# Opening transfers, stage borders and the pace of side work in a two-layer pair kernel

## The chip, the cores and the metric

The kernel runs on one core of one Trainium2 chip. The metric is the device time in microseconds of one execution. Before the change it is 3307.75 us, the median of three runs (3307.7 to 3309.76). The profile was taken in an execution of its own, with a span of 3305.3 us; times of the trace count from the start of that span.

The engines are called as in the profile: PE is TensorE's matrix multiplication and PEld its weight load, DVE is VectorE, ACT is ScalarE, POOL is GpSimd, SP is SyncE, which here only issues transfers. ACT and POOL issue transfers too.

## The reference

The input x is a square table of 384 x 384 positions with 128 channels, in float32. Two layers follow each other.

The first layer is a triangle multiplication. `_layernorm(v, g, b)` subtracts the mean over channels, divides by the root of the variance plus 1e-5, multiplies by g and adds b. Then

```
z     = _layernorm(x, norm_g, norm_b)
left  = (z @ Wl + bl) * sigmoid(z @ Wlg + blg)
right = (z @ Wr + br) * sigmoid(z @ Wrg + brg)
core  = einsum('bikh,bjkh->bijh', left, right)
zo    = _layernorm(core, onorm_g, onorm_b) @ Wout + bout
x1    = x + sigmoid(x @ Wg + bg) * zo
```

so that for each of 128 channels h, `core[:, :, h]` is the product of a 384 x 384 matrix with another one transposed.

The second layer works on each row of the table:

```
left  = x1 @ W_left + b_left + x1 @ W_eq + b_eq
right = sum over the row of (x1 @ W_right + b_right)
out   = (left * right * sigmoid(x1 @ W_gate + b_gate)) @ W_out + b_out
y     = layernorm(out + x1) * ln_scale + ln_bias
```

## The kernel before, in words

One core runs three stages one after the other, with DRAM scratch between them. Within an engine every instruction stays in the order in which the program writes it (`seq`), so one that waits holds up all that stands behind it on its engine. This includes transfers that the engine issues. A transfer in the built program also waits for an earlier one whose completion semaphore it takes over; eight of these go round.

**Stage 1** (to 1140 us) makes `left` and `right` from x. x comes in chunks of 8 rows by 128 positions (`load_chunk`, 512 KB, line 115), with six buffers. A step is 4 rows, half a chunk. Per step, `stats` takes mean and variance on DVE (lines 228, 230), `powers` makes 1/sigma on POOL (243 to 246), `shift` subtracts the mean on POOL (`z`, 253), `front` transposes z on PE (262) and copies it on ACT (`zt`, 264), and `back` does, for two rows at a time, the projection on PE (`pr`, 298) with the 512 columns of the four weight matrices in `wz`, the sigmoid on ACT (305) and the product on DVE (307) into a tile `lr`. Statistics run six steps ahead (`AHEAD`); the first six are written ahead of the first `back`. The transposed x, the negative means and `lr` are stored to DRAM (`xt_d`, `nd_d`, `lr_d`). The last two `lr` tiles stay in SBUF (`kept`).

The opening must make `wz` out of the four weight matrices, the norm's g and b, and the four biases. `fold` (lines 152 to 156) forms d = b - g, multiplies a matrix of 1/128 with it and lets a matmul with the weights add the right sum over rows; `weights` (162) adds that to the scaled weights. The biases are loaded as 128 equal rows of 128 values each. The first two chunks are issued by SP; all weights, columns, biases and the next four chunks by ACT, which then loads its sigmoid table and makes the first `zt`.

**Stage 2** (1140 to 1886 us) does channel after channel, 128 of them. `load_h` brings a channel's left and right interleaved (`lrh`), `fill` takes the right half out on POOL into `rr` (lines 428, 429) and copies the kept parts (432, 433), PE does nine matmuls (449) into three PSUM banks, ACT copies them to `ct` and squares them (458, 459), DVE adds both to the sums `csum` and `csq` over channels (460, 461), and the core goes to `core_d`. `fill` runs one channel ahead. The last channel is special: its first block of 128 rows is finished first, in a bank of its own, so that the inverse deviation of rows 0 to 127 can be made at once: `variance`, `root` (ACT, line 389), `inverse` and `newton` on DVE (393, 403 to 405). Then ACT copies the other two blocks (476), and POOL adds them to the sums (478 to 480).

**Stage 3** (1886 us to the end) goes row by row. For the first 16 rows x is loaded anew (`xn`, line 510) and transposed on PE (575); after that `xt` is loaded as the negative means (`nd_d`, 516) to which POOL's own transfer adds the stored transpose (`add_x`, 524). `front` makes the gate `gT`, `scale_core` the scaled core `cs` (on DVE with a matmul that broadcasts the inverse deviation for rows 0 to 3, lines 597 and 598; on POOL after that, 600, with `rt` loaded from `rstd_d`), `layer0` the first layer's output `x1T`, `gated_left`, `layer1`, `stats1`, `norm1` and `last` the second layer (POOL takes the powers of a pair of rows at line 658 and the last addition at 690). The inverse deviations of rows 128 to 383 are made on the side, in pieces of 128 x 128 (`pieces`): six of variance, two roots taken together, six of inverse and six of Newton. From turn 16 on one is done in every turn t that divides by 5. `add_x` is called whenever 8 rows of lead have been used up.

## Time and profile before

| | |
|---|---|
| time, median of 3 | 3307.75 us |
| span of the profile | 3305.3 us |
| PE busy | 3267.0 us (99%) |
| POOL busy | 2247.9 us (68%) |
| DVE busy | 2495.4 us (75%) |
| ACT busy | 1940.4 us (59%) |
| transfers | 873.96 MB, 264 GB/s on average |

A matmul of float32 appears as two records. A "releaser" in square brackets is what ended an engine's idle time before the instruction, and the number ahead of it how long the engine had been idle. The clock column is the share of full speed that was granted to TensorE; for the first 21 us of the trace it has no entry, and shows 1.00 there whatever it was.

### The profile page before, as it was taken

How to read it: one execution, taken by the hardware profiler on the slowest of the kernel's cores; microseconds unless marked ns; L12 is line 12 of the kernel's file. 1: busy time of each engine (PE TensorE's matmuls, PEld its weight loads, DVE VectorE, ACT ScalarE, POOL GpSimd, SP SyncE). 2: the span in 40 equal slices, each digit the busy share in tenths (PEclk: the TensorE clock that was granted, in tenths of full speed). 3: DMA queues.
4: the chain of work that ended last, by engine and by line, in shares of the span. 5: the costliest groups of instructions: out<-in, count | busy, mean ns of one | idle time of the engine just before them, and what ended most of it. 6: DMA issues, size and time to landing. Idle time of an engine off the chain costs nothing.

```text
span 3305.3 us, 48361 instructions
## 1 busy us (share of the span) xinstructions
PE 3267.0 (99%) x12486; PEld 1992.0 (60%) x12486; DVE 2495.4 (75%) x8041; ACT 1940.4 (59%) x4055; POOL 2247.9 (68%) x3295
## 2 busy tenths in 40 slices
PE   8999999999999999999999999999999999999998
PEld 4544444444444466666666666666777777777776
DVE  6777777777777655555555688888888888888888
ACT  4555555555555433343334467777777777777776
POOL 5555555555555455555555579889888888888887
PEclk9999999999999999999999999999999999999999
DMA  5999999999999499999999999999999999999983
GB/s 151 267 281 268 266 279 272 264 282 271 263 279 275 130 283 283 283 281 283 284 283 282 287 296 267 264 273 276 269 280 270 275 271 276 273 272 277 271 258 113
DMA packets 922818, 873.96 MB, mean 264 GB/s; under 512 B 25008, under 2 KB 837680, under 8 KB 922544
## 3 DMA queue, kind: packets, MB, share of 16 engines
q1 hardware_dynamic: 902480, 794.13, 78.3%
q0 software_dynamic: 13248, 72.36, 11.1%
q10 hardware_dynamic: 6816, 4.39, 0.5%
q8 instruction: 102, 1.67, 0.2%
q14 instruction: 172, 1.41, 0.1%
HBM read 508.89 MB, written 361.89 MB: 263 GB/s over the span
## 4 chain that ended last, share of the span: by engine, by line
PE 62%; POOL 1%; ACT 1%; DVE 1%; issue 0%; POOLq 0%; DVEq 0%; ACTq 0%
PE pc L449 22%; PE py L638 7%; PE pr L609 7%; PE pl L627 7%; PE pg L564 7%; PE pg L626 7%; PE py L639 4%; POOL rs L658 0%; ACT py L673 0%; POOL yt L690 0%; PE pxt L575 0%; PE pq L586 0%; POOL cs L600 0%; DVE st L653 0%; ACT gT L566 0%
## 5 line engine op out<-in xcount | busy, mean ns | idle before, releaser
L298 PE MATMUL pr<-wz,zt 128*128 128x512 f32 x2304 | 1040.3, 593 | 6.2 <-DVE st L228 6.2
L305 ACT ACTIVATE sg<-pr,rs 128x256 f32<-128x256 f32 x1152 | 482.7, 470 | 499.2 <-PE pr L298 365.6
L449 PE MATMUL pc<-rr,lrh 128*128 128x384 f32 x2304 | 745.0, 487 | 2.7 <-POOL rr L428 2.7
L307 DVE SCALAR_TENSOR_TENSOR lr<-pr,rs,sg 128x256 f32<-128x256 f32 x1152 | 505.0, 480 | 267.2 <-ACT sg L305 218.8
L298 PEld LDWEIGHTS pr<-wz,zt 128*128 128x128 f32 x2304 | 414.4, 190 | 417.1 <-issue 346.0
L449 PEld LDWEIGHTS pc<-rr,lrh 128*128 128x128 f32 x2304 | 452.7, 197 | 295.0 <-POOL rr L428 3.3
L673 ACT ACTIVATE py<-py,nm,rs 128x128 f32<-128x128 f32 x1149 | 492.8, 429 | 191.6 <-POOL rs L662 126.9
L638 PEld LDWEIGHTS py<-wo,u 128*128 128x128 f32 x2304 | 377.1, 191 | 100.6 <-DVE yt L684 0.6
L460 DVE TENSOR_TENSOR csum<-csum,ct 128x1152 f32<-128x1152 f32 x127 | 175.6, 1383 | 346.6 <-ACT ct L458 346.6
L600 POOL TENSOR_TENSOR cs<-ct,rt 128x384 f32<-128x384 f32 x380 | 403.7, 1064 | 10.4 <-DMA rt<-rstd_d 9.6
L428 POOL COPY rr<-lrh 128x768 f32<-128x768 f32 x128 | 183.1, 1430 | 329.4 <-DMA lrh<-lr_d 309.2
L458 ACT COPY ct<-pc 128x1152 f32<-128x1152 f32 x127 | 142.1, 1119 | 449.4 <-PE pc L449 449.4
L638 PE MATMUL py<-wo,u 128*128 128x128 f32 x2304 | 402.7, 275 | 0.3 <-ACT wo L620 0.3
L690 POOL TENSOR_TENSOR yt<-yt,lnb 128x384 f32<-128x384 f32 x380 | 400.6, 1056 | 2.1 <-DVE yt L684 2.0
L653 DVE BATCH_NORM_STATS2 st<-py 128x6 f32<-128x128 f32 x1152 | 266.3, 287 | 84.6 <-PE py L639 82.9
L243 POOL TENSOR_SCALAR sd<-mv 128x8 f32<-128x8 f32 (+1 forms) x145 | 28.6, 197 | 436.7 <-DVE mv L230 436.6
L253 POOL TENSOR_TENSOR z<-xt,nd 128x512 f32<-128x512 f32 x288 | 299.8, 1041 | 35.9 <-POOL z L253 30.6
L609 PE MATMUL pr<-cs,wc 128*128 128x384 f32 x768 | 315.1, 492 | 0.1
L627 PE MATMUL pl<-x1T,mat_L_conv_W_left 128*128 128x384 f32 x768 | 311.4, 487 | 3.5 <-ACT gT L566 3.4
L639 PE MATMUL py<-ident,x1T 128*128 128x128 f32 x1152 | 314.0, 273 | 0.0
L626 PE MATMUL pg<-x1T,mat_L_conv_W_gate 128*128 128x384 f32 x768 | 310.8, 486 | 1.2 <-ACT g L629 1.0
L564 PE MATMUL pg<-xt,mat_L_conv_Wg 128*128 128x384 f32 x736 | 298.4, 487 | 0.0
(119 smaller groups left out, 4892.6 us busy)
## 6 DMA issues: line engine op xcount, KB each, us to landing
lr_d<-lr SPq DMA_DIRECT2D x128, 1024.0 KB, 7.1
lrh<-lr_d SPq DMA_DIRECT2D x128, 768.0 KB, 7.8
xt_d<-zt SPq DMA_DIRECT2D x288, 256.0 KB, 5.5
ct<-core_d SPq DMA_DIRECT2D x96, 768.0 KB, 4.8
rt<-rstd_d SPq DMA_DIRECT2D x95, 768.0 KB, 8.4
out_dram<-yt SPq DMA_DIRECT2D x94, 768.0 KB, 7.2
core_d<-ct SPq DMA_DIRECT2D x125, 576.0 KB, 8.9
xt<-in_x_dram SPq DMA_DIRECT2D x140, 512.0 KB, 7.0
```

The lines of the kernel that those rows point to most:

```text
L298: seq(nc.tensor.matmul(pr[:, r, :], lhsT=zts[n, q][:, 2 * half + r, :], rhs=wz, start=True, stop=True))
L305: seq(nc.scalar.activation(sg[r], pr[:, r, 2 * H:], AF.Sigmoid, scale=rs[r]))
L307: seq(nc.vector.scalar_tensor_tensor(t[:, :, c * XR + r0 + r, :], pr[:, r, :2 * H].rearrange("k (h s) -> k h s", s=2), rs[r], sg[r].rearra ...
L449: seq(nc.tensor.matmul(banks[ib], lhsT=t[:, kb, ib * P:(ib + 1) * P, 0], rhs=rr[:, kb], start=(kb == 0), stop=(kb == NB - 1),))
L564: seq(nc.tensor.matmul(pg[:, :N], lhsT=wg0, rhs=r["xT"], start=True, stop=True))
L600: seq(nc.gpsimd.tensor_tensor(cs, ct[:, i % RG], rt[:, i % RG], ALU.mult))
L609: seq(nc.tensor.matmul(pr[:, :N], lhsT=wc, rhs=r["cs"], start=True, stop=True))
L626: seq(nc.tensor.matmul(pg2[:, :N], lhsT=wgate, rhs=r["x1T"], start=True, stop=True))
L627: seq(nc.tensor.matmul(pl[:, :N], lhsT=wleft, rhs=r["x1T"], start=True, stop=True))
L638: seq(nc.tensor.matmul(py[:, s], lhsT=r["u"][:, s], rhs=r["wo"], start=True, stop=False))
L639: seq(nc.tensor.matmul(py[:, s], lhsT=r["x1T"][:, s], rhs=ident, start=False, stop=True, is_transpose=True))
L673: seq(nc.scalar.activation(py[:, s], py[:, s], AF.Identity, bias=bias, scale=scale))
```

## The change

It touches the opening, both borders and the pace of the side work. Its parts:

1. The opening issues transfers in order of need. SP brings half of the first chunk, then g and b as two rows, the other half and chunks 1 to 3; ACT brings the four weight matrices only; the four biases come as single rows, by POOL. Chunks 4 and 5 are loaded after the first step. g and b are turned from rows to columns by a matmul (`pgb`), and the bias is added by a matmul with a single row of 1/128. `fold` moves ahead of the second half of the first step's statistics, `weights` behind the first `shift`. Three matmuls without use (`busy`) keep TensorE at work meanwhile.
2. `fill` copies the kept parts first.
3. At the second border ACT copies the last two blocks ahead of the root, the store of the last channel's first block is split after 16 rows, and the inverse deviation of rows 0 to 127 is stored by POOL ahead of its three operations, no longer by SP.
4. Stage 3 loads the first rows' core as 112 and 16 partitions (channels), ahead of the fourth block of x rows. The two PSUM pools change places, so that the transposes get other banks.
5. Pieces are done in turns with t % 4 = 3 in place of every fifth, and `add_x` from turn 12 on only in turns with t % 4 = 1.

The diff, cut to its core:

```diff
-            for n in range(2):
-                load_chunk(n)
+            load_chunk(0, slice(0, 4))
...
+            for n, v in enumerate(("g", "b")):
+                load(gb[n:n + 1], a["L0_conv_norm_" + v].rearrange("(o h) -> o h", o=1))
             for n, w in enumerate(sides):
                 load(wst[:, n * H:(n + 1) * H], a["L0_conv_W" + w], nc.scalar)
-            g0, b0 = column("L0_conv_norm_g", nc.scalar), column("L0_conv_norm_b", nc.scalar)
-            for n, b in enumerate(sides):
-                load(bst[:, n * H:(n + 1) * H], a["L0_conv_b" + b].partition_broadcast(P), nc.scalar)
-            for n in range(2, 6):
-                load_chunk(n, nc.scalar)
+            load_chunk(0, slice(4, XR))
+            for n in range(1, 4):
+                load_chunk(n)
...
+            for n, b in enumerate(sides):
+                load(brow[:, n * H:(n + 1) * H], a["L0_conv_b" + b].rearrange("(o h) -> o h", o=1), nc.gpsimd)
...
+                busy(2)
+                seq(nc.tensor.matmul(pgb, lhsT=gb, rhs=ident[0:2, 0:2], start=True, stop=True))
+                seq(nc.vector.tensor_copy(g0, pgb[:, 0:1]))
+                seq(nc.vector.tensor_sub(d, pgb[:, 1:2], g0))
                 seq(nc.vector.tensor_scalar(m1, avg, d, None, ALU.mult))
-                seq(nc.tensor.matmul(p1, lhsT=m1, rhs=wst, start=True, stop=True))
-                seq(nc.vector.tensor_scalar(bst, bst, 1.0 / C, None, ALU.mult))
-                seq(nc.vector.scalar_tensor_tensor(wst, wst, g0, bst, ALU.mult, ALU.add))
+                busy(1)
+                seq(nc.tensor.matmul(p1, lhsT=m1, rhs=wst, start=True, stop=False))
+                seq(nc.tensor.matmul(p1, lhsT=avg[0:1, :], rhs=brow, start=False, stop=True))
...
                 for half in range(2):
                     stats(*steps[k], half)
+                    if k == 0 and half == 0:
+                        fold()
                 if k < AHEAD - 1:
                     powers(*steps[k])
                 if k == 0:
-                    fold()
                     zs[0] = shift(*steps[0])
+                    weights()
                     front(*steps[0], zs.pop(0))
...
-                    seq(nc.gpsimd.tensor_copy(rr[:, :NB - 1], t[:, :NB - 1, :, 1]))
-                    seq(nc.gpsimd.tensor_copy(rr[:, NB - 1, :i1], t[:, NB - 1, :i1, 1]))
                     for (kb, ig), lrt in kept.items():
                         i = slice(ig * G, (ig + 1) * G)
                         seq(nc.gpsimd.tensor_copy(t[:, kb, i, 0], lrt[:, h, :, 0]))
                         seq(nc.gpsimd.tensor_copy(rr[:, kb, i], lrt[:, h, :, 1]))
+                    seq(nc.gpsimd.tensor_copy(rr[:, :NB - 1], t[:, :NB - 1, :, 1]))
+                    seq(nc.gpsimd.tensor_copy(rr[:, NB - 1, :i1], t[:, NB - 1, :i1, 1]))
...
-                    seq(nc.scalar.dma_start(out=to[:, 0], in_=ct[:, 0]))
+                    seq(nc.scalar.dma_start(out=to[:16, 0], in_=ct[:16, 0]))
+                    seq(nc.scalar.dma_start(out=to[16:, 0], in_=ct[16:, 0]))
...
+                    seq(nc.scalar.copy(ct[:, 1:], pc[:, 1:, :N]))
                     variance(0, slice(0, N))
                     root(0)
                     inverse(0, slice(0, N))
                     newton(0, slice(0, N))
-                    seq(nc.scalar.copy(ct[:, 1:], pc[:, 1:, :N]))
                     seq(nc.scalar.dma_start(out=to[:, 1:], in_=ct[:, 1:]))
+                    seq(nc.gpsimd.dma_start(out=rstd_d[0:P, :], in_=roots[0][1]))
...
-        ps, ps2 = pool("p3ps", 4, space=PSUM), pool("p3ps2", 4, space=PSUM)
+        ps2, ps = pool("p3ps2", 4, space=PSUM), pool("p3ps", 4, space=PSUM)
...
-                seq(nc.sync.dma_start(out=ct, in_=core_d[i0:i0 + RG].rearrange("i h j -> h i j")))
+                for hs in (slice(0, H),) if i0 > 0 else (slice(0, H - 16), slice(H - 16, H)):
+                    seq(nc.sync.dma_start(out=ct[hs], in_=core_d[i0:i0 + RG, hs].rearrange("i h j -> h i j")))
...
-        for i0 in range(0, 4 * RG, RG):
+        for i0 in range(0, 3 * RG, RG):
             load_x(i0)
         load_core(0)
-        store_rstd(0)
+        load_x(3 * RG)
         load_core(RG)
...
-            if t >= 7 and added <= f + 8:
+            if t >= 7 and (t % 4 == 1 or t < 12) and added <= f + 8:
...
-            if t >= 16 and t % 5 == 0 and pieces:
+            if t >= 16 and t % 4 == 3 and pieces:
```

More of the change, by code (lines that the diff above doesn't have):

```diff
@@ L108, in triangle_then_gated_row_kernel, with load_chunk @@
             lr, full = {}, []
-            def load_chunk(n, queue=nc.sync):
+            def load_chunk(n, part=slice(0, XR)):
                 if n < len(chunks):
@@ L113, in load_chunk @@
                     i0 = ig * G + c * XR
-                    xt = xp.tile([P, XR, C], F32, tag="xt", name="xt")
-                    seq(queue.dma_start(
-                        out=xt, in_=x[i0:i0 + XR, kb * P:(kb + 1) * P, :].rearrange("i k c -> k i c")
-                    ))
-                    loaded[n] = xt
-            for n in range(2):
-                load_chunk(n)
+                    if part.start == 0:
+                        loaded[n] = xp.tile([P, XR, C], F32, tag="xt", name="xt")
+                    src = x[i0:i0 + XR, kb * P:(kb + 1) * P, :].rearrange("i k c -> k i c")
+                    seq(nc.sync.dma_start(out=loaded[n][:, part], in_=src[:, part]))
+            load_chunk(0, slice(0, 4))
             stage = lrp.tile([P, H, G, 2], F32, tag="lr", name="stage").rearrange("p h i s -> p (h i s)")
-            wst, bst = stage[:, 0:4 * H], stage[:, 4 * H:8 * H]
-            m1, d = stage[:, 8 * H:9 * H], stage[:, 9 * H:9 * H + 1]
+            wst, brow, gb = stage[:, 0:4 * H], stage[0:1, 4 * H:8 * H], stage[0:2, 8 * H:9 * H]
+            m1, d = stage[:, 9 * H:10 * H], stage[:, 10 * H:10 * H + 1]
             sides = ("l", "r", "lg", "rg")
+            for n, v in enumerate(("g", "b")):
+                load(gb[n:n + 1], a["L0_conv_norm_" + v].rearrange("(o h) -> o h", o=1))
             for n, w in enumerate(sides):
                 load(wst[:, n * H:(n + 1) * H], a["L0_conv_W" + w], nc.scalar)
-            g0, b0 = column("L0_conv_norm_g", nc.scalar), column("L0_conv_norm_b", nc.scalar)
-            for n, b in enumerate(sides):
-                load(bst[:, n * H:(n + 1) * H], a["L0_conv_b" + b].partition_broadcast(P), nc.scalar)
-            for n in range(2, 6):
-                load_chunk(n, nc.scalar)
-            ident = const([P, P], "ident")
-            make_identity(nc, ident)
+            load_chunk(0, slice(4, XR))
+            for n in range(1, 4):
+                load_chunk(n)
             avg = const([P, P], "avg")
@@ L141, in triangle_then_gated_row_kernel @@
             seq(nc.vector.memset(mhalf, -0.5))
+            ident = const([P, P], "ident")
+            make_identity(nc, ident)
+            for n, b in enumerate(sides):
+                load(brow[:, n * H:(n + 1) * H], a["L0_conv_b" + b].rearrange("(o h) -> o h", o=1), nc.gpsimd)
             warm = const([P, 1], "warm")
@@ L146, in triangle_then_gated_row_kernel, with busy @@
             p1 = pps.tile([P, 2, 4 * H], F32, tag="pr", name="p1")[:, 0]
+            pgb = tps.tile([P, 4, P], F32, tag="pt", name="pgb")[:, 0, 0:2]
+            g0 = const([P, 1], "g0")
+            def busy(n):
+                for _ in range(n):
+                    seq(nc.tensor.matmul(
+                        p1, lhsT=avg, rhs=avg.unsqueeze(1).to_broadcast([P, 4, P]), start=True, stop=True
+                    ))
             def fold():
-                seq(nc.vector.tensor_sub(d, b0, g0))
+                busy(2)
+                seq(nc.tensor.matmul(pgb, lhsT=gb, rhs=ident[0:2, 0:2], start=True, stop=True))
+                seq(nc.vector.tensor_copy(g0, pgb[:, 0:1]))
+                seq(nc.vector.tensor_sub(d, pgb[:, 1:2], g0))
                 seq(nc.vector.tensor_scalar(m1, avg, d, None, ALU.mult))
-                seq(nc.tensor.matmul(p1, lhsT=m1, rhs=wst, start=True, stop=True))
-                seq(nc.vector.tensor_scalar(bst, bst, 1.0 / C, None, ALU.mult))
-                seq(nc.vector.scalar_tensor_tensor(wst, wst, g0, bst, ALU.mult, ALU.add))
+                busy(1)
+                seq(nc.tensor.matmul(p1, lhsT=m1, rhs=wst, start=True, stop=False))
+                seq(nc.tensor.matmul(p1, lhsT=avg[0:1, :], rhs=brow, start=False, stop=True))
             def weights():
@@ L161, in weights @@
                     gs = slice(g * 2 * H, (g + 1) * 2 * H)
-                    seq(nc.vector.tensor_add(
+                    seq(nc.vector.scalar_tensor_tensor(
                         wz[:, gs].rearrange("p (h s) -> p s h", s=2),
-                        wst[:, gs].rearrange("p (s h) -> p s h", s=2),
-                        p1[:, gs].rearrange("p (s h) -> p s h", s=2),
+                        wst[:, gs].rearrange("p (s h) -> p s h", s=2), g0,
+                        p1[:, gs].rearrange("p (s h) -> p s h", s=2), ALU.mult, ALU.add,
                     ))
@@ L328, in triangle_then_gated_row_kernel @@
                 if k == 0:
-                    fold()
                     zs[0] = shift(*steps[0])
+                    weights()
                     front(*steps[0], zs.pop(0))
                 if k == 1:
-                    weights()
                     zs[1] = shift(*steps[1])
@@ L351, in triangle_then_gated_row_kernel @@
                 store_zt(n, q)
+                if k == 0:
+                    for i in range(4, 6):
+                        load_chunk(i)
                 store_slice()
```

## The prediction

> **What bounds the kernel now.** I read the busy shares first, then the idle time of TensorE (PE) in stretches, then the timelines where it is idle.

> ```profile
> PE 3267.0 (99%) x12486; PEld 1992.0 (60%) x12486; DVE 2495.4 (75%) x8041; ACT 1940.4 (59%) x4055; POOL 2247.9 (68%) x3295
> ```

> TensorE is idle for 3305.3 - 3267.0 = 38.3 us in all, so only those microseconds, and matmuls that run at a reduced clock, are to be had. The stretches show where they lie (columns: stretch, its length, then busy time and count of each engine, granted clock, DMA share, GB/s):

> ```profile
> 0.00:20.00 20.00, 4.96 (x9) 2.38 (x10) 7.41 (x41) 1.96 (x3) 6.00 (x16) 1.00 0.72 187
> ...
> 1120.00:1150.00 30.00, 27.27 (x79) 13.93 (x78) 11.82 (x25) 11.97 (x27) 8.35 (x18) 0.94 0.25 74
> ...
> 1870.00:1900.00 30.00, 27.60 (x103) 17.62 (x102) 21.53 (x22) 16.50 (x25) 11.98 (x15) 0.94 0.93 292
> ...
> 2000.00:2100.00 100.00, 97.38 (x466) 68.00 (x465) 84.47 (x302) 74.14 (x171) 86.50 (x121) 1.00 0.92 266
> 2100.00:2300.00 200.00, 198.22 (x948) 139.46 (x947) 175.06 (x615) 144.03 (x334) 178.52 (x253) 1.00 0.94 272
> ...
> 3280.00:3306.00 26.00, 11.97 (x72) 9.03 (x71) 18.12 (x67) 13.47 (x33) 13.77 (x22) 0.78 0.30 91
> ```

> Idle: 15.0 us in the opening, 2.7 at the first border (stage 1 to 2), 2.4 at the second, 2.6 + 1.8 early in stage 3, 13.3 in the tail, which the change leaves alone. Everywhere else TensorE is full. In the timeline of the opening (start, duration, engine, line), watch what the first projection (L298) waits for:

> ```profile
> 5.42 0.49 DVE L228 BATCH_NORM_STATS2 st<-xt 128x6 f32<-128x128 f32 x2 [4.40 <-DMA xt<-in_x_dram]
> ...
> 8.30 7.62 ACTq L115 DMA_DIRECT2D xt<-in_x_dram  x4
> ...
> 14.43 0.43 DVE L155 TENSOR_SCALAR stage<-stage 128x512 f32<-128x512 f32 x1 [5.63 <-DMA stage<-in_L_conv_brg_dram]
> ...
> 15.95 1.28 ACT L144 ACT_TABLE_LOAD   x1 [15.95 <-DMA xt<-in_x_dram]
> ...
> 17.35 0.57 ACT L264 COPY zt<-pt 128x512 f32<-128x512 f32 x1
> ...
> 17.97 3.55 PE L298 MATMUL pr<-wz,zt 128*128 128x512 f32 x4 [6.20 <-DVE st L228]
> ```

> Two things end together: ACT's queue is full of transfers until 15.9 us, so its first table load and `zt` copy come after them, and the broadcast bias arrives at 14.4, which delays `wz`. Then 4 records take 3.55 us where 8 take 3.60 four microseconds later: the clock is at half.

> At the second border (timeline), ACT copies the last two blocks only behind the root that it waits for, and the transposes wait for that copy:

> ```profile
> 1886.65 0.52 ACT L389 ACTIVATE r<-ve 128x384 f32<-128x384 f32 x1 [2.15 <-DVE ve L385]
> 1887.08 0.78 ACT L476 COPY ct<-pc 128x768 f32<-128x768 f32 x1
> ...
> 1887.91 2.55 PE L575 MATMUL pxt<-ident,xn 128*128 128x128 f32 x12 [2.40 <-ACT ct L476]
> ...
> 1889.79 1.79 DVE L403 TENSOR_TENSOR r<-m 128x384 f32<-128x384 f32 x1
> ```

> [...] granted clock 0.50 for some 3.4 us after each border's idle, and the slow first projections above. [...] L403 takes 1.79 us beside POOL's L479, and L405, of the same size after POOL is done, 0.56. [...] small columns from SP land in 2.1 to 2.2 us later in stage 1, in 5.0 in the crowded opening.

> **The opening.** Here is the new chain, from the rates before. By 5.0 us 0.78 MB had moved (19, 108, 327, 323 GB/s in the microseconds from 1 to 5). A half chunk (256 KB) with one weight matrix is 0.33 MB, reached at 3 + (0.33 - 0.13)/0.327 = 3.6; I take 3.8 for the first statistics, against 5.42. Meanwhile PE runs two dummies, cold, at 1.78 us each (the 3.55 for two above), from 1.1 to 4.7; `pgb` to 5.0; g0, d, m1 on DVE (0.1 + 0.16 + 0.29, plus hand-overs) to 5.75; the second half's statistics to 6.4; the powers on POOL 1.9 (6.79 to 8.66 before) to 8.35; z 1.04 to 9.45. The four weights and the second half chunk make 0.78 MB, so they land by 5 to 5.8. The bias rows: four issues on POOL of about 0.9 us each (L524's median 0.91) from 1.3 to 5[...]. The upper end is 10, with the 5.0 that small transfers took in the opening before. The fold's two matmuls then end between 8 (warm, 0.9 each) and 10.4 (cold), `wz` 0.8 later; DVE holds it for nothing else. ACT is free since 3 us, its table loaded. So transposes at 9.6, `zt` at 11, first projection at 11 to 12.3. The second step's statistics now stand behind `wz` on DVE: 1.3 + powers 1.9 + z 1.04 bring the second transposes to end at 14.4 (warm) to 16.6 (cold), where they ended at 21.96: 5.4 to 7.6 us, and I take **6.6**. Late bias rows (10 us) leave 3; everything warm and early gives 8. Chunks 1 to 3 (1.5 MB at about 0.3 MB/us after 8) land by 13, ahead of the statistics that want them. Nothing after it can take the gain back easily: TensorE is full from 20 us to 1137 with DMA at 0.91.

> **First border.** Kept copies first puts three POOL copies of 0.18 us (one of the four has no wait and goes early) ahead of the `rr` copy at 1139.58 that the first stage-2 matmul waits for: **+0.5** (0 to +0.9). In the rest of stage 2 they end before the transfer lands; hidden by TensorE's 5.8 us per channel. Their other effect: the x rows of stage 3 no longer wait for the last of them (1879.43), but for copies that are ready a channel earlier, so their transfers start about 4 us sooner.

> **Second border.** The PSUM pools change places, so the transposes take banks that channel 126 left at 1880.9: they can follow the last matmul (1885.5) at once, no idle and no cold window. ACT copies the last blocks at 1885.6 to 1886.4, before the root, which was waiting for DVE until 1886.65 anyhow; so the root costs nothing, and `xT` copies start at about 1887.6 instead of 1888.63. The first `pg` comes at 1888.15 against 1890.25; at 0.975 us a row (1.48 + 0.56 + ... settles at 1892.90 to 1893.88) four rows end at 1892.05. DVE must have done Newton by then: POOL's three operations now stand behind the rstd store, which waits for `r`, so DVE is alone and takes 2.55 (the reciprocal before) + 3 x 0.56, 1887.2 to 1891.5 instead of 1894.26. `pb` at 1893.3 instead of 1895.92. The core of rows 0 to 3 for 112 channels no longer waits for the last channel's store, and 16 partitions wait for 16 rows of it: about 1890 against 1897.4. So **-2.6** (0.5 if x rows or core come late, 3.5 at best). The rstd store through POOL queues sq, csum and csq behind it (5.4 us); who needs them are row 19's pieces. The first POOL `cs` (row 4) may slip by 5 us before a matmul waits for it.

> **Early stage 3.**

> ```profile
> PE pl L627 <- ACT gT L566: 3.4, 4, 1.5
> ...
> PE pg L626 <- ACT g L629: 1.0, 1, 1.0
> ```

> The first are at 2031, 2093, 2182 and 2265, where the chain runs through POOL's powers (L658, 1.34), `yt`, the x transfer's issue (0.9) and `cs`: the same turns in which a piece every 5 and the transfer every 4 coincide (every 20th). Afterwards pieces come at t % 4 = 3, transfers at t % 4 = 1, powers on even turns: they never coincide, and I take 3.0 of 3.4 as gone. The 1.0 is the square root's table change (1.28 twice and 0.94 at 2065), which stays. Cost: POOL's load. It is busy 562 of 650 us (86%) without pieces; a Newton piece is 0.46 + 0.30 + 0.46 = 1.2 per 4 rows of 3.6 us, 8.5%: 95% in that stretch, under full. **-3.0** (-4.4 to +2).

> **Sum.** -6.6 + 0.5 - 2.6 - 3.0 = -11.7: 3307.75 - 11.7 = **3296.0**.

> **Rivals.** (a) Late bias rows and waits that only move: -3.0 + 0.5 - 2.6 + 0 = -5.1, 3302.6. For it: no small POOL transfer is in the trace, and POOL nears 95%. Against: the bias has 2 to 3 us of slack behind z. (b) All at their ends: -8.0 + 0 - 3.5 - 4.4 = -15.9, 3291.9. For it: the dummies may warm the clock before the fold; against: PE is idle again for 1 to 2 us behind the fold, which can cool it. (c) Slower: POOL becomes the bound while there are pieces, and each of about 19 turns pays its whole 1.2 us: 19 x 1.2 = +22.8, with DMA (0.91) taking the opening's gain back, +0.5 - 2.6: 3328.5. For it, POOL's 178.5 of 200 us already; against, that these were busy turns with waits of only 1.8 us.

> **How the numbers follow.** Forecast 0.58, (a) 0.22, (b) 0.13, (c) 0.07. 0.2% is 6.6 us, so the line is 3301.1: (a) falls within it mostly; faster 0.58 + 0.13 + 0.07 of (a) = 0.78, same 0.15, slower 0.07. The range, 3291.5 to 3303, holds the forecast, most of (a) and of (b).

> **What would show it.** First projection at 11 to 12.3; its duration tells the clock. `rr` copy at the first border later by 0.5. No PE wait on ACT's copy at the second border, and no 0.50 clock there; L403's successor at 0.56. No waits on `gT` in the 400 us after. Wrong if the bias rows land after 10, if the transposes wait for x rows, or if POOL's idle time before 2300 vanishes and `cs` or `yt` turns up as releaser of TensorE.

## The result, and the profile after

The changed kernel takes 3298.58 us (median of 6 runs, 3298.19 to 3300.16) beside 3308.14 for the one before (6 runs, 3307.66 to 3309.76): ratio 0.9971, 95% interval 0.9958 to 0.9984, 9.56 us faster. Taken again with the experiments, on another chip, it was 3298.22 (15 runs, 3294.9 to 3301.24) beside 3306.1: ratio 0.9976, interval 0.9968 to 0.9984. The profile shown here is of the slowest of the first six runs (3300.16 us, span 3298.4), and the one of before is of an execution of 3307.08 us. So the two profiles differ by 6.9 us, where the medians differ by 9.56: readings by the profile show less gain than the typical run has.

The same stretches as before, but for the tail (stretch, length, busy time and count of each engine, granted clock, DMA share, GB/s):

```profile
0.00:20.00 20.00, 17.00 (x39) 7.30 (x40) 12.22 (x69) 5.61 (x11) 13.87 (x30) 0.91 0.86 223
1120.00:1150.00 30.00, 26.73 (x77) 14.41 (x76) 12.29 (x19) 11.10 (x21) 10.21 (x23) 0.94 0.41 123
1870.00:1900.00 30.00, 28.81 (x114) 17.77 (x113) 20.94 (x35) 16.65 (x29) 11.01 (x9) 1.00 0.96 308
2000.00:2100.00 100.00, 98.61 (x467) 68.39 (x466) 86.77 (x306) 75.91 (x174) 88.45 (x123) 1.00 0.96 265
2100.00:2300.00 200.00, 199.21 (x950) 139.71 (x949) 174.57 (x615) 144.94 (x335) 179.35 (x251) 1.00 0.98 272
```

PE's idle time of 15.0, 2.7, 2.4 and 4.4 us is now 3.0, 3.3, 1.2 and 2.2. (In the first stretch PE's busy time includes the three dummies.) The second border has lost its half clock: 1.00 where 0.94 stood. The opening runs much as the forecast had it (start, duration, engine, line):

```profile
3.97 0.49 DVE L241 BATCH_NORM_STATS2 st<-xt 128x6 f32<-128x128 f32 x2 [2.95 <-DMA xt<-in_x_dram]
...
7.37 1.12 PE L169 MATMUL p<-stage,avg 1*128 1x512 f32 x2
...
8.53 0.87 DVE L175 SCALAR_TENSOR_TENSOR wz<-stage,g,p 128x256 f32<-128x256 f32 x2 [2.04 <-PE p L169]
...
10.98 3.12 PE L311 MATMUL pr<-wz,zt 128*128 128x512 f32 x4 [0.68 <-ACT zt L277]
...
13.90 1.06 PE L275 MATMUL pt<-ident,z 128*128 128x128 f32 x4
```

The matmul with the bias row (L169) follows the one before it without a wait, so the rows that POOL issued from 1.46 us on were there in time. And the second border, VectorE's timeline and two lines of TensorE's: no Newton step is above 0.56 us, and `pb`, the broadcast of the inverse deviation, starts at 1886.87. One wait on ACT's copy is left there, 0.56 us ahead of the transposes of the second row.

```profile
1880.07 1.20 PE L598 MATMUL pxt<-ident,xn 128*128 128x128 f32 x9 [0.56 <-ACT ct L490]
1880.88 2.55 DVE L410 RECIPROCAL m<-r 128x384 f32<-128x384 f32 x1 [0.59 <-ACT r L406]
1883.46 0.56 DVE L420 TENSOR_TENSOR r<-m 128x384 f32<-128x384 f32 x1
1884.06 0.56 DVE L421 SCALAR_TENSOR_TENSOR r<-r,ve 128x384 f32<-128x384 f32 x1
...
1886.87 0.81 PE L620 MATMUL pb<-r,ident 128*128 128x384 f32 x2
```

In the profile of before, `pb` started at 1895.92:

```profile
1895.92 0.81 PE L597 MATMUL pb<-r,ident 128*128 128x384 f32 x2
```

**Where the time went.** I compared the start of the same instruction in both traces along the program. Stage 1 runs 6.87 us ahead from its third row to its last, stage 2 6.33, the first rows of stage 3 9.00. Row 8 is 9.27 ahead. Then something new takes time back: row 12 is only 5.42 ahead. By row 110 it is 7.8, at the last row 7.5, at the end 6.9. Three lines of the list of what TensorE waits for (total us, times, longest); in the kernel before, no wait on `cs` stands there. POOL's timeline tells what is behind it:

```profile
PE pc L466 <- POOL rr L449: 3.3, 1, 3.3
PE pr L632 <- POOL cs L623: 1.9, 1, 1.9
PE pl L650 <- ACT gT L589: 1.3, 5, 0.3
```

```profile
1905.37 2.37 POOL L623 TENSOR_TENSOR cs<-ct,rt 128x384 f32<-128x384 f32 x2
1916.79 0.88 POOL L545 DMA_DIRECT2D xt<-xt_d  x1 [9.05 <-DMA xt<-nd_d]
1917.40 3.20 POOL L623 TENSOR_TENSOR cs<-ct,rt 128x384 f32<-128x384 f32 x3
```

POOL has to issue its third accumulating transfer, which waits 9.05 us for the load of its tile. The scaled core `cs` of the coming rows stands behind it on POOL, and TensorE waits 1.89 us. In the kernel before POOL waited almost as long for the same transfer, and TensorE did not:

```profile
1922.27 0.88 POOL L524 DMA_DIRECT2D xt<-xt_d  x1 [8.17 <-DMA xt<-nd_d]
```

After the wait, in the changed kernel, the clock drops (stretch, PE busy, granted clock, DMA share, GB/s):

```profile
1919.00:1920.00 1.00, 1.00 (x4) 0.87 0.96 363
1920.00:1923.00 3.00, 3.00 (x10) 0.50 1.11 315
1923.00:1924.00 1.00, 1.00 (x7) 0.92 1.05 264
```

3.4 us at half clock are another 1.7 us: 1.9 + 1.7 = 3.6 of the 3.85 us that are lost between rows 8 and 12.

### The profile page after: what moved, and what is told of

Its sections match the earlier page's. It is cut to its first block, busy times and chain, and to the rows that moved or that the text cites. A ratio compares the mean times of both kernels' runs of the same rounds, so it can differ in the third digit from the quotient of the medians.

```text
span 3298.4 us, 48398 instructions
## 1 busy us (share of the span) xinstructions
PE 3272.9 (99%) x12496; PEld 1993.3 (60%) x12496; DVE 2492.5 (76%) x8040; ACT 1944.1 (59%) x4055; POOL 2291.5 (69%) x3300
## 4 chain that ended last, share of the span: by engine, by line
PE 95%; POOL 2%; DVE 1%; ACT 1%; DMA 1%; issue 1%; POOLq 0%; ACTq 0%; DVEq 0%
PE pr L311 30%; PE pc L466 23%; PE py L661 7%; PE pr L632 7%; PE pg L587 7%; PE pl L650 7%; PE pg L649 7%; PE pt L275 4%; PE py L662 3%; POOL cs L623 1%; POOL rs L681 1%; DMA xt<-nd_d 1%; POOL yt L713 1%; ACT py L696 0%; DVE st L676 0%
## 5 line engine op out<-in xcount | busy, mean ns | idle before, releaser
L623 POOL TENSOR_TENSOR cs<-ct,rt 128x384 f32<-128x384 f32 x380 | 427.7, 1129 | 4.9 <-DMA rt<-rstd_d 4.9
L713 POOL TENSOR_TENSOR yt<-yt,lnb 128x384 f32<-128x384 f32 x380 | 424.8, 1119 | 3.4 <-DVE yt L707 3.4
```

The source lines that it names most:

```text
L623: seq(nc.gpsimd.tensor_tensor(cs, ct[:, i % RG], rt[:, i % RG], ALU.mult))
L713: seq(engine.tensor_tensor(yt, yt, lnbb, ALU.add))
```

## Experiments

Each ratio is to the kernel before on the same chip; its median was 3306.14 in the first group (e1 to e4), 3306.1 in the second (the changed kernel again, e5, e6, e9) and 3306.53 in the third (e7, e8, e10, e11). "Ahead" is by the profile against that of before. A "turn" is one pass of stage 3's loop. In the expectations the "cosine product" is `cs`, the scaled core, and the "relative bank" is `pr`, the bank that TensorE fills from it.

**The parts alone.** Three kernels are the one before with some of the parts: the opening (part 1), the borders (parts 2 to 4), the pace (part 5).

```
e1: before + part 1          e2: before + parts 2, 3 and 4          e3: before + part 5
```

> The kernel before with part 1 of the change alone, the opening. Theory (the parts add up, each in its own stretch): the last projection of stage 1 comes 6.9 us earlier than before, and the whole is 6 to 7 us shorter, about 3301.5. Rival (a shorter opening is partly given back later, to transfers or to the first border): less than 4 us are left at the end. A wait of TensorE on the scaled core at rows 10 to 12 of stage 3 is not expected here.

> The kernel before with parts 2, 3 and 4 alone: kept copies first, the second border, core load and PSUM pools. Theory: first border 0.5 later, second border 2.7 earlier, so that first rows of stage 3 come 2.2 us earlier; then the wait at rows 10 to 12 that the changed kernel shows (1.9 us and a window at half clock, 3.6 together) comes with these parts, and the whole is between 2.2 us faster and 1.4 slower. Rival (that wait comes from the pace of the side work, part 5): no such wait here, 2.2 us faster plus or minus 0.5.

> The kernel before with part 5 alone, the pace of pieces and of the transfers that POOL issues. Theory: TensorE's waits between 2000 and 2300 us fall from 4.4 us to some 2, the whole gets 2 to 2.5 us shorter, about 3305.7. Rival (waits only move, POOL is near full): within 0.7 us of before. Second rival (part 5 makes the wait at rows 10 to 12): that wait shows here.

Measured: opening 3300.2 (0.9982, interval 0.9975 to 0.9989), -5.9 us. Borders 3308.82 (1.0008, 0.9999 to 1.0016), +2.7. Pace 3304.07 (0.9994, 0.9985 to 1.0002), -2.1. The last two intervals just include no change; of the single runs, 12 of e2's 13 lie above the median of before, and all 13 of e3's below it. So the opening is most of the gain. The borders alone cost more than the 1.4 us that had been allowed, although in e2's trace they give what was forecast: border 1 costs 0.54, border 2 gives 2.69. Between rows 8 and 12 it then loses 4.62, by the new wait (2.67) and a half-clock stretch (1.7); e1 and e3 have neither there. The wait belongs to the borders' part. The parts sum to -5.3 and the whole, taken again in the second group, is -7.9; 0.8 of the difference is that between rows 8 and 12 the whole loses 3.85 and e2 4.62. I can't place the rest. Within the opening and within the pace (pieces and transfers) the single edits were not separated, but for the dummies below.

```profile
PE pr L615 <- POOL cs L606: 2.7, 1, 2.7
```

(from e2's list of waits). The kernels that keep the old opening (e2, e3 and e8) stand 0.7 to 1.5 us ahead of the profile of before already in stage 1: that profile opened late. Against its fellows the changed kernel's 6.87 are 5.4 to 6.2, which agrees with e1's 5.9.

**The dummies.**

```diff
-                busy(2)
...
-                busy(1)
```

> The changed kernel without the three matmuls without use in the opening. Theory (they only bring the clock up for the fold): the fold's two matmuls take 1.8 us each in place of 1.1, the second transposes end 1 to 2 us later, and the whole is 1 to 2 us longer. Rival 1 (they do nothing, the fold has slack): within 0.3 us at the last projection of stage 1. Rival 2 (the opening's gain is mostly the warm clock): 4 us or more.

Measured: 3300.4 (0.9984, 0.9977 to 0.999). Stage 1 is 5.39 ahead, 1.5 less than with dummies, as the theory had it. The fold's two matmuls take 2.04 and 2.07 us in place of 1.10 and 1.12, which is about the ratio of half clock to full (the trace has no clock entry this early), and the first projection starts at 12.41 in place of 10.98:

```profile
6.65 2.04 PE L166 MATMUL p<-stage 128*128 128x512 f32 x2 [1.83 <-DMA stage<-in_L_conv_Wrg_dram]
8.62 2.07 PE L167 MATMUL p<-stage,avg 1*128 1x512 f32 x2
...
12.41 3.59 PE L309 MATMUL pr<-wz,zt 128*128 128x512 f32 x4 [0.67 <-DVE st L239]
```

**The changed kernel again, and two ways out of the new wait.** e5 calls the third accumulating transfer three turns later, in turn 13 in place of 10. e6 gives the store of 1/std back to SyncE and holds POOL behind Newton with a copy of one column into a tile that nothing else needs any more.

```diff
 e5:
-            if t >= 7 and (t % 4 == 1 or t < 12) and added <= f + 8:
+            if t >= 7 and (t % 4 == 1 or t < 10) and added <= f + 8:
 e6:
-                    seq(nc.gpsimd.dma_start(out=rstd_d[0:P, :], in_=roots[0][1]))
+                    seq(nc.gpsimd.tensor_copy(warm, roots[0][1][:, 0:1]))
...
         load_x(3 * RG)
+        store_rstd(0)
```

> The changed kernel itself, taken again beside the three that follow so that they can be compared on one chip. Both theories: as in its first profile, stage 1 some 6.9 us earlier than before, border 1 0.5 later, border 2 2.7 earlier, and 3.6 us lost again by the twelfth row of stage 3 (a wait of 1.9 us of the relative bank on the cosine product of POOL, then a half-clock stretch). By the parts run singly (-6.0, +2.7, -2.0 us) it would come to 5.3 us below the kernel before; by its first runs 9.6.

> The changed kernel with the third accumulating x transfer called at iteration 13 in place of 10 of stage 3, nothing else. Theory A (POOL stands 9 us at that transfer's wait for the load of its tile, and the cosine product is queued behind it): TensorE's 1.9 us wait on POOL's cosine product is gone, the half clock after it too, the twelfth row starts 9.0 us earlier than in the kernel before instead of 5.4, and the time falls by 2 to 3.6 us. Theory B (the cosine product itself comes late because its rstd rows are reloaded late, whoever is ahead of it): at most 0.5 us changes. Theory C (the new pace of the accumulating transfers matters only further on): no change at row 12, under 0.5 us in the time.

> The changed kernel with the store of 1/std put back to SyncE's queue behind the first x load, as before, and POOL held behind the reciprocal by a copy of one column in its place. Theory A/B (the store from POOL takes some 3 us longer until its reader can start, so that the x and rstd loads of stage 3 come about 3 us later): the rstd rows and the x tile of the third transfer land 2 to 3 us sooner, the wait of 1.9 us on the cosine product goes and the half clock with it, the time falls by 2 to 3.6 us; the border keeps its 2.7 us. Theory C (the issuing engine does not matter, the loads are slow because the DMA engines are full): loads land at the same time within 0.7 us and the time within 0.5 us of the changed kernel.

Measured: 3298.22 again, e5 3295.98 (0.997, 0.9959 to 0.9982), e6 3296.77 (0.9971, 0.996 to 0.9982). The intervals overlap with that of the changed kernel, but 13 of its 15 runs on this chip lie above all six of e5. In e5 the wait and the half clock are gone: rows 0 and 12 are 9.1 and 9.3 ahead. POOL goes on with `cs` and issues the third transfer at 1923.00 without waiting:

```profile
1906.05 4.48 POOL L623 TENSOR_TENSOR cs<-ct,rt 128x384 f32<-128x384 f32 x4
...
1923.00 0.94 POOL L545 DMA_DIRECT2D xt<-xt_d  x1
```

Theories B and C fall: `cs` itself was not late. For e6 neither theory was right. The wait is gone, but the reload of 1/std is issued at 1891.80, in the changed kernel at 1891.79:

```profile
1891.80 0.33 SPq L559 DMA_DIRECT2D rt<-rstd_d  x1
...
1915.39 0.89 POOL L545 DMA_DIRECT2D xt<-xt_d  x1 [6.66 <-DMA xt<-nd_d]
```

From the store to its reader it took 5.4 us from SyncE here, against 6.3 from POOL in the changed kernel. It was 3.2 (e8) to 6.9 us (e9) from SyncE, and from POOL 6.3 to 6.6 to the landing (changed kernel twice, e5), so whether the issuing engine counts stays open; in e6 it brought nothing. What helped: the third transfer could start 1.4 us sooner (1915.39), and the rows came 1.2 us later, since the first border had a second half-clock stretch (below). That stretch was luck. Without it, by the sums below, some 0.5 us of the wait would have been left (an estimate: 2.20 + 1.2 - 2.87).

The profiles where that transfer is called in turn 10 obey one line. Take the time from the start of row 8's first layer on VectorE to the issue of that transfer:

```
changed kernel      4.75   wait 1.9        before            0.96   none
the same again      4.83   wait 2.0        e1 opening        2.52   none
e2 borders          5.54   wait 2.7        e3 pace           1.36   none
e4 no dummies       4.61   wait 1.7        e6 store by SP    2.20   none
e7 old fill order   5.20   wait 2.3        e8 banks only     1.10   none
                                           e11 no hold       1.41   none
```

The wait is this time less 2.87, within 0.05 us, in all five; and below 2.87 there is none. This is what an in-order queue must give when the rows keep one pace; it shows how much time each kernel has to spare. In the kernel before 1.9 us were left. The change takes them: row 8 starts 9.3 us earlier, the transfer only 5.5. Why the load can't follow, whether by the full DMA engines (a mean share of 0.96 to 1.11 from 1919 to 1924 us, above) or by the order in which transfers follow one another on their semaphores (in the opening of before, SyncE's first store of `xt_d` waits 6.6 us for the load of the bias `bl`, eight transfers ahead of it in the program), was not separated.

**Both, with the old fill order at the first border alone.**

```diff
 e5's and e6's edits, and in fill():
+                    def whole():
...
+                    if h == 0:
+                        whole()
                     for (kb, ig), lrt in kept.items():
...
+                    if h > 0:
+                        whole()
```

> The changed kernel with both of these edits and with the old order of the fill (whole groups first, kept operands behind) at the first border alone. Theory A: the first border's wait on the fill falls from 3.3 to 2.7 us, the twelfth row of stage 3 has no wait on POOL; together 2.5 to 4.1 us below the changed kernel. Rival: stage 3 gives the gain back further on, because TensorE meets its waits on the gated rows sooner; under 1 us.

Measured: 3295.23 (0.9965, 0.9952 to 0.9979), the fastest kernel here, 3.0 below the changed one, though not to be told from e5. The first border's wait is 2.7 as expected, but the second gives 1.8 in place of 2.7: VectorE's `cs` of the first row starts only at 1888.95, after 1.72 us of idle time. `pb`, which the view names for it, had ended at 1887.28, so it waited for something else.

```profile
1888.95 1.02 DVE L627 TENSOR_TENSOR cs<-ct,pb 128x384 f32<-128x384 f32 x2 [1.72 <-PE pb L626]
```

**What makes the second border.** e7 has the old fill order everywhere; e8 is the kernel before with only the PSUM pools in changed places; e11 is e6 without the one-column copy.

```diff
 e8:
-        ps, ps2 = pool("p3ps", 4, space=PSUM), pool("p3ps2", 4, space=PSUM)
+        ps2, ps = pool("p3ps2", 4, space=PSUM), pool("p3ps", 4, space=PSUM)
 e11, against e6:
-                    seq(nc.gpsimd.tensor_copy(warm, roots[0][1][:, 0:1]))
```

> The changed kernel with the old order of the fill everywhere (whole groups first, kept operands behind them), nothing else. Theory A (kept first costs three small copies at the first border and frees the x rows of stage 3 earlier at the second): stage 2 starts 0.5 us sooner than in the changed kernel, the first x transfers of stage 3 are issued some 4 us later, and at the second border the first transposes or gated rows wait, 0.5 to 2 us; together 0 to 1.5 us slower. Rival (the early x transfers are not needed, since the banks alone decide when the transposes start): border 2 unchanged, 0.5 us faster.

> The kernel before with only the two PSUM pools of stage 3 in changed places. Theory A (the idle time and the half clock of the second border are the banks' doing, but the end of the border is set by Newton on VectorE and the core's landing): the wait of 2.4 us on ACT's last copy goes and the half clock with it, but the broadcast of 1/std comes no earlier than before and TensorE waits there, so that the rows are at most 1 us ahead at row 4. Rival (banks are all of it): rows 2.0 to 2.7 us ahead, the whole gain of the second border.

> The changed kernel with the store of 1/std on SyncE's queue as before and nothing that holds POOL: its three operations on the last two blocks start when ACT's copy ends and lie beside Newton's steps on VectorE. Theory A[...]: Newton's three steps of 0.56 us become longer by 1.2 to 2.5 us in sum, the first broadcast of 1/std comes 1 to 2.5 us later than in the run where POOL was held, and 0.5 to 2 us of the second border's 2.7 are lost. Rival: the steps stay at 0.56 us and the border keeps its 2.7 us; the hold was worth nothing.

Measured: e7 3296.7 (0.9971, 0.9959 to 0.9982), e8 3306.41 (0.9999, 0.9991 to 1.0007), e11 3297.9 (0.9973, 0.9962 to 0.9983). At the second border e8 gains 0.0 us. The transposes of the first row now start behind the last matmul, but the bank of the second row is still in use, and the wait moves there, 2.08 us. The half clock stays as well (0.94 from 1870 to 1900), against both theories. `pb` comes behind Newton, no sooner than before when the 1.35 us are counted that e8 is ahead all along:

```profile
1884.00 0.49 PE L575 MATMUL pxt<-ident,xn 128*128 128x128 f32 x3
1886.57 1.61 PE L575 MATMUL pxt<-ident,xn 128*128 128x128 f32 x9 [2.08 <-ACT ct L476]
...
1894.58 0.81 PE L597 MATMUL pb<-r,ident 128*128 128x384 f32 x2
```

e11 gains 1.1 in place of 2.7. The first Newton step lies beside POOL again:

```profile
1883.26 2.11 DVE L420 TENSOR_TENSOR r<-m 128x384 f32<-128x384 f32 x1
1885.40 0.56 DVE L421 SCALAR_TENSOR_TENSOR r<-r,ve 128x384 f32<-128x384 f32 x1
```

So holding POOL is worth 2.11 - 0.56 = 1.55 us, which is 2.67 - 1.12. While the step of 2.11 us ran, POOL added to `csq` (1883.14 to 1884.94); the next one, from 1885.40 on, had no POOL operation beside it and took 0.56. In the trace of before the two steps beside POOL's additions took 1.79 and 2.05 us, and the third, behind them, 0.56. e7 gains 1.9 at the second border, 0.8 less than the changed kernel, since VectorE's `cs` waits 1.7 us for the core:

```profile
DVE cs L621 <- DMA ct<-core_d: 1.7, 1, 1.7
```

But e9 has the kept-first order there, gives 1.8 all the same, and has the same idle time ahead of `cs`. So the 0.8 can't be put on the order of the fill; why the core comes late in these two is open. What is shown is its cost of 0.54 at the first border. e7 had been expected to be up to 1.5 us slower than the changed kernel, and it is 9.8 below its own before, where the changed kernel was 7.9 below. No half clock at the first border, as its profile shows, fits that, but one profile doesn't prove it of the other runs.

**A better first border and opening?** e10 is e5 with the copies of the first fill that take out the right half on VectorE (the kept parts stay on POOL), and one more dummy between `weights` and the first transposes.

```diff
                     weights()
+                    busy(1)
                     front(*steps[0], zs.pop(0))
...
+                    eng = nc.vector if h == 0 else nc.gpsimd
...
+                    seq(eng.tensor_copy(rr[:, :NB - 1], t[:, :NB - 1, :, 1]))
+                    seq(eng.tensor_copy(rr[:, NB - 1, :i1], t[:, NB - 1, :i1, 1]))
```

> The changed kernel with the third accumulating transfer at iteration 13, with the first fill of stage 2 on VectorE in place of POOL, and with one more dummy between the weights and the first transposes. Theory: the first border's wait falls from 3.3 us to 2.0 to 2.7 (VectorE holds the last products, so no hand-over, and its copies are shorter); the dummy fills the 1.0 us of idle ahead of the transposes, the clock stays full through the first projections and stage 1 comes 0.3 to 0.9 us sooner. 0.8 to 2 us below the kernel with the third transfer alone. Rival: the dummy only pushes the transposes back by 0.2 us and the first projection is held by the next rows anyway, so nothing in the opening; VectorE's strided copies are as slow as POOL's, so nothing at the border.

Measured: 3297.55 (0.9975, 0.9965 to 0.9985), 9.0 below its own before, where e5 was 10.1 below; by the medians the two are not to be told apart. By the profile both edits missed: stage 1 is 6.1 ahead in place of e5's 6.9, and border 1 costs 1.8 in place of 0.5. VectorE copies faster (0.49 + 0.32 us against POOL's 0.86 + 0.40), but its copies stand behind two memsets of 1.02 us, and TensorE waits 4.6:

```profile
1133.53 1.02 DVE L433 MEMSET csum<- 128x1152 f32 x1 [0.19 <-issue]
1134.74 1.02 DVE L434 MEMSET csq<- 128x1152 f32 x1 [0.19 <-DVE csum L433]
1135.68 0.49 DVE L451 COPY rr<-lrh 128x768 f32<-128x768 f32 x1
...
1136.27 4.17 PE L468 MATMUL pc<-rr,lrh 128*128 128x384 f32 x7 [4.61 <-issue]
```

The dummy writes the bank that `wz` reads, so it waits for `wz` and pushes the transposes from 9.60 to 11.70.

## Why the prediction was right, and where not

Forecast 3296.0, measured 3298.58: the direction and most terms held. The forecast was 11.7 us less than before; the first runs give 9.6 less, the second group 7.9.

**Opening, -6.6:** 6.87 by the profile, 5.9 by the medians of e1; the 6.87 have some luck in them, since the profile of before opened late. Most steps held: statistics at 3.97 (3.8), first projection at 10.98 (11 to 12.3), second transposes to 14.96 (14.4 to 16.6). From 11.68 us on the first projections ran at half clock again (3.12 us for 4 records), after 1.84 us of idle between 8.26 and 11.67. Rival (a)'s late bias rows didn't come: the last landed at 6.76. How soon a small row that POOL issues lands was not shown by the trace of before; here the issues took 0.49 to 0.76 us in place of 0.9, and the rows landed 2.9 to 3.8 us after them. (The column that took 5.0 in the opening of before, the prediction's upper end, was issued by ACT, not by SP.)

**First border, +0.5:** 0.54. **Second border, -2.6:** 2.67, mostly by the steps named. The banks did less than was said. Only the first row's transposes follow the last matmul at once; the second row's wait 0.56 us for ACT's copy, which now comes early because it stands ahead of the root. e8 shows that the bank swap buys nothing alone; what it is worth beside the other edits was not tested. e11 puts 1.55 on POOL's hold. That the core no longer waits for the last store was not tested by itself.

**Early stage 3, -3.0:** 2.2 by the idle time, 2.1 by e3. Waits on `gT` stayed, five short ones (1.3 us in sum), where none were expected.

**The step that failed** is "The first POOL `cs` (row 4) may slip by 5 us before a matmul waits for it." It asked about the three operations behind the store, and TensorE indeed doesn't wait for these. It did not ask about the next thing on POOL that waits: `add_x`, whose 8.17 us wait in the trace of before was harmless by 1.9 us. Moving the rows 9 us ahead of a load that follows by 5.5 made it bind: +3.6 in the profile (1.9 of wait, 1.7 of clock), +2.2 by the medians of e5 and the changed kernel. The last paragraph of the prediction names this sign, `cs` as releaser, but the sum had no term for it.

The measured terms add up: the opening is 0.7 short of its forecast, early stage 3 is 0.9 short, and the missing term costs 2.2, so -11.7 becomes -7.9, which is what the second group shows. Why the first runs, on another chip, were 1.7 better than that is open. With the third transfer moved (e5) the gain is 10.1 of the 11.7. That e5's time, 3295.98, is the very number of the forecast is luck: before was 1.65 us faster on that chip than the 3307.75 from which the forecast counts.

## What to carry to other kernels

When a change brings work forward, list every wait of before on an in-order queue that cost nothing, with the time it had to spare, and ask whether what it waits for comes forward as far. A transfer that can be issued later is better issued when its operand has landed than in front of compute. And a short stall of TensorE can cost nearly twice its length, since the clock may fall with it (1.89 us of wait, then 1.7 of clock), or no more than its length (1.74 us in e4).

## What the runs showed of the hardware

**The half-clock stretches of these traces lie on a grid.** In the changed kernel they begin at 11.68, 1134.68 and 1919.74 us (from the mean clock of the microsecond in which each begins: 0.84 means 0.32 us at half):

```profile
11.00:12.00 1.00, 1.00 (x2) 0.84 0.26 68
...
1134.00:1135.00 1.00, 0.83 (x2) 0.84 1.14 203
```

Each lasts 3.40 to 3.42 us by the same reckoning. The distances between their starts are 1123.00 and 785.06 us; 1123.00 / 329 and 785.06 / 230 both give 3.413, so they fit whole multiples of one length, which is that of the stretches (worked out from these numbers). From the stretch in the opening to the one at the first border it is 1122.98 to 1123.00 us in e1, e5, e8, e9, e11 and the changed kernel taken again too, and 1126.40, one stretch more, in e10. A "window" is from here on 3.413 us, counted from the start of a half-clock stretch. An idle time of about 3 us cost 0, 1 or 2 windows at half clock, each 1.7 us. At the first border (idle 3.3 us in e5 and e6, 2.7 in e7):

```profile
1120.00:1150.00 30.00, 26.73 (x76) 0.94 0.41 121
```

```profile
1120.00:1150.00 30.00, 26.74 (x72) 0.89 0.36 115
```

```profile
1120.00:1150.00 30.00, 27.26 (x84) 1.00 0.47 144
```

(e5, e6, e7 in this order: one window, two, none). In the kernel before and in e9 the 2.7 us cost one window.

| where | window begins (us) | idle in it (us) | clock in the next |
|---|---|---|---|
| e4, row 10 | 1916.92 | 1.74 | 1.00 |
| changed kernel, row 10 | 1916.33 | 1.89 | 0.50 |
| e8, second border | 1883.80 | 2.08 | 0.50 |
| e6, first border | 1129.86 | 2.50 | 0.50 |
| e5, first border | 1131.09 | 3.03 | 0.50 |

So a window with little more than half of it idle was enough. In e7 a wait of 2.74 us at the first border and one of 2.3 us at row 10 did no harm to the clock (1.00 from 1120 to 1150 and from 1900 to 1930). That each lay across two windows, with less than 1.89 us in either, would explain it; this is an estimate from the other thirteen. Between the opening and the tail, a window at half clock was followed by one at full clock in all cases but one: the first of e6's two had 0.76 us of idle in it, and the next stayed at half. In the opening, windows with 1.0 us (e10) and 1.8 us of idle (changed kernel) were followed by half clock as well, so there the 1.74 us doesn't hold.

A difference of one or two times 1.7 us between two single profiles can therefore come without any effect of an edit; only the medians, or the idle time, tell. It may also be why the 15 runs of the changed kernel spread over 6 us, since its wait of 1.9 us is just long enough to fill a window by half; the runs without a profile show no clock by place, so that stays a guess.
